# Two attention blocks in fp32 on one core: a fourth convolution in halves twice, the projection straight after attention, and statistics moved

## The chip, the cores and the metric

The program runs on one core of a Trainium2 chip. The core has a matrix engine (TensorE, PE in the profile), three engines for elementwise work (VectorE or DVE, ScalarE or ACT, GpSimd or POOL), a sequencer that issues transfers (SyncE, SP), and 16 DMA engines that its queues share. Each engine takes its instructions in the order of its own queue and waits on semaphores for the others. The metric is the device time of one execution in microseconds (us), here a median over ten executions.

## The reference

The input is a batch of 8 images, each 512 channels by 1024 positions (32 x 32), in fp32. Two attention blocks follow each other:

```python
# layer 0: group norm (32 groups), 8 heads of 64 channels
h   = group_norm(x)
qkv = w_qkv @ h + b_qkv                     # [1536, 1024] per image
weight = softmax((q * s).T @ (k * s))       # per head, [1024, 1024]
a   = weight @ v                            # back to [512, 1024]
x   = x + w_proj @ a + b_proj
# layer 1: group norm (8 groups), one head of 512 channels
xn  = group_norm(x)
q, k, v = q_w @ xn + q_b, k_w @ xn + k_b, v_w @ xn + v_b
attn = softmax(q.T @ k / sqrt(512))         # [1024, 1024]
out  = attn @ v
x    = x + p_w @ out + p_b
```

All that matters here is matrix products of 512 x 512 weights with 512 x 1024 images, the attention products, and the elementwise work between them.

## The kernel before

**Products by halves.** A product of two matrices that are each cut into 2 x 2 blocks is made from seven block products instead of eight, with sums of blocks before and after (`wino`, L227; its seven products carry the numbers 1 to 7). `left_sums` (L151) and `right_sums` (L165) make the sums of the two factors: eight subtractions or additions of 128 x 512 for one image. The weights' sums are made once in the prologue and kept in DRAM (`prepare`, `keep`), and each use reads them back with `load_weight` (1.79 MB) into one of three buffers, three uses ahead in the list `uses`. In `wino`, step p does the matmuls of product p (4 of 128 x 128 by 512 columns for a weight product) and then reads the accumulator that is complete: 1, 2, 5, 6 and 7 run in the order of `middle`, and steps 4 and 3 are put into the list `tail`, which the next product runs behind its own step 1 (`finish`), so that the accumulators of one product are read while the next product's first matmuls run.

**Halves twice.** Two convolutions of layer 0, for keys and queries, go one level further (`conv2`, L416): each of the seven products is itself made from seven, so 49 matmuls of 256 columns take the place of 28 of 512 columns. The inner sums of the image are made by POOL (`inner_factors`, L400; 28 subtractions of 128 x 256, L411), the inner sums of the weights once in the prologue by POOL (`keep2`, L296: four operations of 128 x 896 and seven transfers). `conv2` runs in four groups (`pair`) of products: (1,5), (2,6), (7) and (3,4). In each group the inner steps go 1, 6, 2, 5, 7, and the inner steps 3 and 4 run behind the next group's step 1. Each result is an addition of an accumulator and an earlier result on DVE (`add`, L439); `more` (L444) adds on POOL what product 7 gives to two places. An accumulator holds several results one after the other: step 7 adds onto the accumulator that step 6 left, so its matmuls wait until DVE has read it (the buffer `u`), step 3 onto that of step 5 (buffer `c`), and step 4 onto that of step 7.

**Names in the profile.** The tiles are named by stage: `g` is layer 1's first convolution (the weights `m` are the product of layer 1's query and key weights, made in the prologue), `p` layer 0's projection, `sc` and `av` the scores and the weighted values, `z` layer 1's second convolution, `v`, `k`, `q` layer 0's three convolutions. `psa_`, `psb_`, `psc_` are their accumulators (PSUM), `h` and `t_h` a normed image and its sums, `inner_h` the sums of sums, `a` and `t_a` the output of layer 0's attention and its sums, `bnst` the statistics of a norm.

**The order of the stages.** The loop over images (L928) software-pipelines the two layers. For image b of 1 to 7 it runs: layer 0's attention of image b (`attention0`, L577: eight blocks, one for each pair of heads and half of the queries), then layer 1's first convolution `g` of image b-1, the projection of image b (`projection`), layer 1's scores, `z` and weighted values of image b-1, and layer 0's `v`, `k` and `q` of image b+1. For image 0 it is attention, then image 1's `v`, the projection of image 0, and image 1's `k` and `q`. After the loop, layer 1 of the last image runs alone.

**One attention block** is eight score products, each followed by an exponential on ACT (L594) and, from the second on, by an addition of 128 x 1024 on DVE into the sum (L596, L598); then sixteen products with the values (`av`); then a matmul of the sum with ones (`sums`, L557), which waits for the last of the seven additions, since PE's queue is in order, and the next block's products wait behind it. DVE takes the reciprocal (L559); a row of it goes to DRAM and comes back broadcast (`rows` and `r`, both on SP's queue), and POOL scales the block's output with it (L615). The last block's scaling is done by DVE (`scaled`, L617) inside the stage that follows.

**What sets the order.** Matmuls keep the program's order (L67). On the other engines a scheduler orders what is not pinned by `tc.keep_in_program_order`. The list `background` holds small elementwise steps which `wino` and `conv2` take out between their own steps (`run_background`); the lists `hooks`, `extra` and `later` put steps at given places. The norm of layer 1 takes its statistics inside the projection: `residual` adds the projection to the image (L845, L847), and puts `bn_stats` (L98, eight of 128 x 512 for an image) and `bn_aggr` (L103, four) into `background`; the group's mean and variance go over PE (`gmean`, `gvar`) between the steps of the scores.

Of the kernel before, what the change touches and what calls it, by code (L numbers as in the profile page):

```python
# [29 lines left out]
def two_attention_blocks_kernel(  # L30
# [145 lines left out]
    def main_path(ctx):  # L176
# [117 lines left out]
        wdram2 = {n: dram.tile([P, 7, 7, P], F32, name=f"sums2_{n}") for n in "qk"}  # L294

        def keep2(n, t):  # L296
# [5 lines left out]
            for dst, x, y, op in (  # L302
                (s1, a21, a22, ALU.add), (s2, s1, a11, ALU.subtract), (s3, a11, a21, ALU.subtract),
                (s4, a12, s2, ALU.subtract),
            ):
                nc.gpsimd.tensor_tensor(dst, x, y, op)
# [3 lines left out]
        twice = [("k", 0), ("k", 1), ("q", 0), ("q", 1)]  # L310
        uses = ["v", "p", *twice] if B > 1 else ["p"]
        for b in range(1, B):
            uses += ["m", "p", "z"] + (["v", *twice] if b + 1 < B else [])
# [3 lines left out]
        def load_weight():  # L317
            if uses:
                n = uses.pop(0)
                t = wpool.tile([P, 7 * C], F32, tag="w", name=f"w_{n[0]}_{len(uses)}")  # L320
                if n in twice:
# [18 lines left out]
        def image_factors(h, uid):  # L340
# [5 lines left out]
                [lambda j, t=t: t[:, j, :] for t in tiles], nc.vector.tensor_sub,  # L346
# [69 lines left out]
        def conv2(n, f, bias, name, hooks=(), late=None):  # L416
# [123 lines left out]
            last = [lambda: biased_half(0, 1), lambda: biased_half(1, 0)]  # L540
# [3 lines left out]
            pair(3, (3, 4), [(0, 1), (1, 0)], [(0, 1), (1, 0)], [load_weight, *last])  # L544
# [3 lines left out]
        def reciprocals(total, uid, across):  # L548
# [14 lines left out]
            nc.sync.dma_start(rows.rearrange("j i n -> i j n"), rc[0:P:32, :, :])  # L563
            if across:
                r = pair_tile(f"r_{uid}")
                for j in range(2):
                    row = rows[j : j + 1].rearrange("j i n -> j (i n)")
                    nc.sync.dma_start(r[:, j, :], row.to_broadcast([P, HT]))
            else:
                r = rpool.tile([P, HT], F32, tag="r", name=f"r_{uid}")  # L570
                for j in range(2):
                    row = rows[j : j + 1].rearrange("j i n -> j (i n)")
                    nc.sync.dma_start(r[ts(j, 64), :], row.to_broadcast([64, HT]))
# [3 lines left out]
        def attention0(b, q, k, v, extra):  # L577
            a = channel_tiles(f"a0_{b}")
            n = 0
            for hp in range(KC):  # L580
                for tb in range(2):
# [31 lines left out]
                    r = reciprocals(total, uid, False)  # L613
                    if (hp, tb) != (KC - 1, 1):
                        nc.gpsimd.tensor_tensor(dst, dst, r, ALU.mult)  # L615
                    else:
                        scaled = lambda dst=dst, r=r: nc.vector.tensor_mul(dst, dst, r)  # L617

            assert not extra
            return a, scaled  # L620
# [131 lines left out]
        def prologue():  # L752
# [45 lines left out]
            for n in "pmz":  # L798
                t, steps = prepare(n)
                later.append(steps)  # L800
                later.append([lambda n=n, t=t: keep(n, t), load_weight])
# [5 lines left out]
            return v, q, k, norm1, later  # L807

        psum_pools("first", 2)
        v, q, k, norm0, later = prologue()  # L810
# [23 lines left out]
        def attention_steps(a, scaled, b):  # L834
            af, steps = image_factors(a, f"a_{b}")
            return af, [[], [scaled, lambda: background.extend(steps)]]

        def projection(b, af, xt):

            norm = GroupNorm(1, f"1_{b}")  # L840

            def residual(i, r, c, ps, u):
                oc = 2 * r + i
                xh = xt[oc][:, ts(c, HT)]
                nc.vector.scalar_tensor_tensor(xh, ps, obias[0][:, oc : oc + 1], xh, ALU.add, ALU.add)  # L845
                if u is not None:
                    nc.vector.tensor_add(xh, xh, u)  # L847
                background.append(lambda: norm.half_stats(oc, c, xh))

                if c == 1 - r:  # L850
                    background.append(lambda: norm.end_stats(oc))
# [6 lines left out]
            by_channel(weight("p"), af, f"p_{b}", residual, after=[load_weight, store])  # L858
            return norm

        def norm_hooks(norm, uid):
            return [
                [], [], [all_background], [lambda: norm.group_mean(acc_tile(f"gmean_{uid}")[:, :KC])],
# [28 lines left out]
        def layer1_scores(b, h, hooks):  # L892
            hf, steps = image_factors(h, f"h1_{b}")
            background.extend(steps)
            g = conv(
                weight("m"), hf, ubias, f"g1_{b}", middle=(2, 5, 6, 7), hooks=hooks, back=4,
                after=[load_weight, lambda: background.extend(gsteps)],
            )
# [6 lines left out]
            return hf, gf  # L905

        def layer1_rest(b, hf, gf, hooks, ahead):
            e, total, ef = scores1(b, gf, hf, f"1_{b}", hooks)
# [19 lines left out]
        for b in range(B):  # L928
# [11 lines left out]
            for i, f in enumerate(applies):  # L940
                extra[2 * i + 3].append(f)
            if b > 0:
                extra[0] += late
            psum_pools(f"attention_{b}", 1)
            a, scaled = attention0(b, q, k, v, extra)
            psum_pools(f"products_{b}", 2)
            xt = [load_x(b, c, "x") for c in range(KC)]
            af, ends = attention_steps(a, scaled, b)
            if b > 0:
                hf, gf = layer1_scores(b - 1, h, ends)  # L950
                norm1 = projection(b, af, xt)
# [9 lines left out]
            elif B > 1:  # L961
                v, f, norm0 = values(1, h, ends)
                norm1 = projection(0, af, xt)
                q, k, late = keys_and_queries(1, f, norm0, norm_hooks(norm1, "1_0")[1:])
            else:
                for f in sum(ends, []):
                    f()
                all_background()
                norm1 = projection(0, af, xt)
                finish()  # L970
                for f in sum(norm_hooks(norm1, "1_0"), []):
# [4 lines left out]
        hf, gf = layer1_scores(B - 1, h, ())  # L976
# [197 lines left out]
```

## Time and profile before

| | |
|---|---|
| median of 10 executions | 2904.65 us (2902.1 to 2908.01) |
| the profiled execution's own time | 2907.18 us |
| its span in the trace | 2905.4 us |
| granted TensorE clock | 0.999 |
| PE busy | 2888.4 us (99%) |
| DVE busy | 1936.9 us (67%) |
| ACT busy | 872.7 us (30%) |
| POOL busy | 468.2 us (16%) |
| DMA moved | 267.97 MB, mean 92 GB/s |

Busy time is time with at least one instruction in flight on the engine. A matmul's end is modelled, so PE's records overlap a little, and a matmul that starts late behind a wait can lie in the shadow of the one before. The chain of waits is the chain that ended last, followed back from the last instruction; what stands in it is on the path that sets the end. Matmuls of fp32 appear as two records each. The stages of one image of the loop can be told apart in the trace by their tiles: for image 1, attention ends at 452.1 us, and `g`, `p`, the scores, `z`, `av`, `v`, `k` and `q` end at 690 us, where the next image's attention begins.

### The profile page before, as it was taken

The numbers are of one execution on the slowest core, as the hardware profiler recorded it, in microseconds if no ns is written. First come the engines' busy times: TensorE is split into PE (matmuls) and PEld (weight loads), VectorE is DVE, ScalarE is ACT, GpSimd is POOL, SyncE is SP. The second block draws the span as 40 slices with busy tenths as digits, with TensorE's granted clock in tenths as the row PEclk, the third lists the DMA queues.
The fourth block names the chain that finished last, engine by engine and source line by source line (L and its number), as shares of the span: only waits on it lengthen the run. The fifth ranks groups of instructions, "written<-read, shape, count | busy, mean of one in ns | idle before, by whom it ended". The sixth has DMA issues, their size and how long they took to land.

```text
span 2905.4 us, 29024 instructions
## 1 busy us (share of the span) xinstructions
PE 2888.4 (99%) x10838; PEld 1499.5 (52%) x10838; DVE 1936.9 (67%) x2613; ACT 872.7 (30%) x1117; POOL 468.2 (16%) x525
## 2 busy tenths in 40 slices
PE   9999999999999999999999999999999999999999
PEld 5435634566345653457534574346733458334544
DVE  5488787556765668665786567866577665776555
ACT  1251452114512055121551115411164112631110
POOL 3013210032200322003210122102121031110000
PEclk9999999999999999999999999999999999999999
DMA  8432402133032231222312232122411223011201
GB/s 277 156 133 92 175 19 93 68 123 132 19 112 87 87 126 48 83 92 95 116 47 81 92 135 77 48 80 95 149 62 44 80 103 146 30 55 69 91 3 66
DMA packets 84186, 267.97 MB, mean 92 GB/s; under 512 B 10371, under 2 KB 29891, under 8 KB 75974
## 3 DMA queue, kind: packets, MB, share of 16 engines
q1 hardware_dynamic: 83622, 265.89, 25.3%
q8 instruction: 87, 1.43, 0.2%
q14 instruction: 61, 0.50, 0.1%
q10 hardware_dynamic: 416, 0.16, 0.0%
HBM read 216.30 MB, written 49.72 MB: 92 GB/s over the span
## 4 chain that ended last, share of the span: by engine, by line
PE 98%; DVE 2%; DMA 0%; issue 0%; ACT 0%; SPq 0%; DVEq 0%
PE sc L67 15%; PE av L67 15%; PE psb_sc L67 6%; PE psb_av L67 6%; PE psa_av L67 4%; PE psa_sc L67 4%; PE psc_av L67 4%; PE psc_sc L67 4%; PE psb_p L67 3%; PE psb_z L67 3%; PE psb_g L67 3%; PE psb_v L67 3%; PE psb_k L67 3%; PE psb_q L67 2%; PE psa_v L67 2%; PE psa_z L67 2%
## 5 line engine op out<-in xcount | busy, mean ns | idle before, releaser
L598 DVE TENSOR_TENSOR sum<-sum,e 128x1024 f32<-128x1024 f32 x384 | 519.1, 1352 | 40.4 <-DVE sum L598 0.5
L594 ACT ACTIVATE e<-sc 128x1024 f32<-128x1024 f32 x512 | 476.8, 1050 | 72.8 <-PE sc L67 72.8
L67 PE MATMUL sc<-q,k 64*128 64x512 f32 x2048 | 458.3, 596 | 0.0
L67 PE MATMUL av<-e,v 128*64 128x512 f32 x2048 | 453.6, 595 | 0.0
L67 PEld LDWEIGHTS sc<-q,k 64*128 64x128 f32 x2048 | 192.3, 186 | 239.2 <-ACT e L594 110.1
L67 PEld LDWEIGHTS av<-e,v 128*64 128x64 f32 x2048 | 141.4, 137 | 304.3 <-issue 302.3
L561 POOL TENSOR_TENSOR all_recs<-all_recs,rc 128x256 f32<-128x256 f32 x72 | 64.5, 896 | 883.2 <-DVE rc L559 883.2
L559 DVE RECIPROCAL rc<-sums 128x256 f32<-128x256 f32 x72 | 126.4, 1756 | 89.3 <-PE sums L67 87.0
L615 POOL TENSOR_TENSOR a<-a,r 128x512 f32<-128x512 f32 x56 | 109.3, 1952 | 270.9 <-DMA r<-rows 251.7
L646 ACT ACTIVATE e<-e 128x512 f32<-128x512 f32 x96 | 60.5, 630 | 232.6 <-DVE e L645 232.6
L612 ACT COPY a<-av 128x512 f32<-128x512 f32 x64 | 37.5, 586 | 304.9 <-PE av L67 304.9
L596 DVE TENSOR_TENSOR sum<-e,e 128x1024 f32<-128x1024 f32 x64 | 78.5, 1226 | 60.2 <-ACT e L594 60.2
L67 PE MATMUL psa_sc<-g,h 128*128 128x512 f32 x256 | 115.7, 594 | 0.0
L67 PE MATMUL psa_av<-e,z 128*128 128x512 f32 x256 | 113.3, 595 | 0.0
L128 POOL TENSOR_TENSOR rstd<-ve,mhalf 128x4 f32<-128x4 f32 x16 | 16.7, 1044 | 499.6 <-DVE ve L126 499.6
L140 ACT ACTIVATE h<-h,b,s 128x1024 f32<-128x1024 f32 x62 | 78.5, 1270 | 60.9 <-DMA h<-in_x 48.3
L67 PEld LDWEIGHTS psa_sc<-g,h 128*128 128x128 f32 x256 | 48.1, 190 | 57.9 <-issue 56.2
L67 PEld LDWEIGHTS psa_av<-e,z 128*128 128x128 f32 x256 | 48.0, 190 | 57.3 <-issue 55.2
L67 PE MATMUL psb_k<-inner_h,w_k 128*128 128x256 f32 x294 | 75.3, 383 | 0.0
L67 PE MATMUL psb_q<-inner_h,w_q 128*128 128x256 f32 x294 | 74.9, 383 | 0.0
L249 ACT COPY t_sc<-psa_sc 128x512 f32<-128x512 f32 x32 | 18.7, 586 | 181.7 <-DVE x L847 152.4
L444 POOL TENSOR_TENSOR k<-k,k 128x256 f32<-128x256 f32 x28 | 20.1, 728 | 297.0 <-DVE u_k L439 297.0
(304 smaller groups left out, 4584.4 us busy)
## 6 DMA issues: line engine op xcount, KB each, us to landing
x<-in_x SPq DMA_DIRECT2D x36, 512.0 KB
h<-in_x SPq DMA_DIRECT2D x32, 512.0 KB
r<-rows SPq DMA_DIRECT2D x128, 128.0 KB
spill<-x SPq DMA_DIRECT2D x32, 512.0 KB
h<-spill SPq DMA_DIRECT2D x32, 512.0 KB
x<-spill SPq DMA_DIRECT2D x32, 512.0 KB
out<-x SPq DMA_DIRECT2D x64, 256.0 KB
w_p<-sums_p SPq DMA_DIRECT2D x8, 1792.0 KB
```

Source lines behind the costliest of these rows:

```text
L67: tc.keep_in_program_order(nc.tensor.matmul(*args, **kw))
L140: tc.keep_in_program_order(nc.scalar.activation(dst, src, AF.Identity, bias=b, scale=s))
L249: nc.scalar.copy(t1[i], ps["a", i])
L444: nc.gpsimd.tensor_tensor(d, x, y, ALU.add)
L559: nc.vector.reciprocal(rc, sums)
L561: nc.gpsimd.tensor_tensor(all_recs, all_recs, rc, ALU.add)
L594: nc.scalar.activation(e, sc, AF.Exp, scale=(C // 8) ** -0.5)
L596: nc.vector.tensor_add(total, es[0], e)
L598: nc.vector.tensor_add(total, total, e)
L612: nc.scalar.copy(dst, av)
L615: nc.gpsimd.tensor_tensor(dst, dst, r, ALU.mult)
L646: nc.scalar.activation(dst, dst, AF.Exp, scale=scale)
```

## The change

`m` joins `k` and `q` among the weights with sums of sums, and `g` of images 0 to 6 is made by `conv2`; the last image keeps the plain form. The order after the attention of image b becomes projection of image b, `g` of image b-1, scores. The projection's `middle` becomes (5, 6, 7, 2).

The projection needs all of attention's output soon, so the last pair's two blocks swap, and the block that ends last is (3, 0): its half is part of what products 2 and 4 need, and its scaling (`scaled`) and one last sum come behind step 7. That block's `rows` and `r` transfers go on ACT's queue. The sums of attention's output are pinned and mostly made inside attention's last two blocks. The sums of layer 1's image (`image_factors` of `h1`), which DVE made around the beginning of `g`, are spread over blocks 4 to 7 of attention, and their inner sums (28 operations on POOL) are issued when attention is over, so that they run beside the projection.

The statistics of layer 1's norm are pinned, collected in a list, and put into `background` after the second group of `conv2`; the means and variances move one step earlier in the scores. In `conv2` the last two biased halves swap.

In image 0 the inner sums of the weights `m` are made by `keep2`, now pinned on POOL, after the first attention (`more_later`), followed by the load of `p`, and the statistics of image 0 are taken in image 1's `k`.

```diff
-        wdram2 = {n: dram.tile([P, 7, 7, P], F32, name=f"sums2_{n}") for n in "qk"}
+        wdram2 = {n: dram.tile([P, 7, 7, P], F32, name=f"sums2_{n}") for n in "qkm"}
         def keep2(n, t):
...
-                nc.gpsimd.tensor_tensor(dst, x, y, op)
+                tc.keep_in_program_order(nc.gpsimd.tensor_tensor(dst, x, y, op))
...
         for b in range(1, B):
-            uses += ["m", "p", "z"] + (["v", *twice] if b + 1 < B else [])
+            uses += ["p", *twice["m"], "z"] + (["v", *twice["k"], *twice["q"]] if b + 1 < B else [])
...
-            pair(3, (3, 4), [(0, 1), (1, 0)], [(0, 1), (1, 0)], [load_weight, *last])
+            pair(3, (3, 4), [(0, 1), (1, 0)], [(0, 1), (1, 0)], [load_weight, *last, *after])
...
-        def attention0(b, q, k, v, extra):
-            a = channel_tiles(f"a0_{b}")
+        def attention0(b, q, k, v, a, extra):
...
-                for tb in range(2):
+                for tb in (0, 1) if hp < KC - 1 else (1, 0):
...
-                    r = reciprocals(total, uid, False)
-                    if (hp, tb) != (KC - 1, 1):
+                    last = (hp, tb) == (KC - 1, 0)
+                    r = reciprocals(total, uid, False, nc.scalar if last else nc.sync)
+                    if not last:
                         nc.gpsimd.tensor_tensor(dst, dst, r, ALU.mult)
...
-            norm = GroupNorm(1, f"1_{b}")
+            norm = GroupNorm(1, f"1_{b}", pinned=True)
+            stats, rest = [], []
...
-                background.append(lambda: norm.half_stats(oc, c, xh))
+                stats.append(lambda: norm.half_stats(oc, c, xh))
                 if c == 1 - r:
-                    background.append(lambda: norm.end_stats(oc))
+                    stats.append(lambda: norm.end_stats(oc))
...
+            by_channel(
+                weight("p"), af, f"p_{b}", residual, middle=(5, 6, 7, 2), hooks=[[], [], hooks, [], [add_rest]],
+                after=[load_weight, store],
+            )
+            return norm, stats
...
-        def layer1_scores(b, h, hooks):
-            hf, steps = image_factors(h, f"h1_{b}")
-            background.extend(steps)
-            g = conv(
-                weight("m"), hf, ubias, f"g1_{b}", middle=(2, 5, 6, 7), hooks=hooks, back=4,
-                after=[load_weight, lambda: background.extend(gsteps)],
-            )
+        def layer1_scores(b, hf, inner, hooks):
+            after = [lambda: background.extend(gsteps)]
+            if inner:
+                g = conv2("m", inner, ubias, f"g1_{b}", hooks, after)
+            else:
+                g = conv(weight("m"), hf, ubias, f"g1_{b}", middle=(2, 5, 6, 7), back=4, after=[load_weight, *after])
...
         def layer1_rest(b, hf, gf, hooks, ahead):
+            finish()
             e, total, ef = scores1(b, gf, hf, f"1_{b}", hooks)
...
+            a = channel_tiles(f"a0_{b}")
+            af, steps = image_factors(a, f"a_{b}", lambda *t: tc.keep_in_program_order(nc.vector.tensor_sub(*t)))
+            extra[13] += steps[:2]
+            extra[15] += steps[2:4]
             if b > 0:
                 extra[0] += late
+                hf, sums = image_factors(h, f"h1_{b - 1}")
+                for i in range(4):
+                    extra[9 + i] += sums[2 * i : 2 * i + 2]
...
             if b > 0:
-                hf, gf = layer1_scores(b - 1, h, ends)
-                norm1 = projection(b, af, xt)
+                inner, sums2 = inner_factors(hf, f"h1_{b - 1}")
+                for f in sums2:
+                    f()
+                norm1, stats = projection(b, af, xt, [scaled, steps[7]])
+                gf = layer1_scores(b - 1, hf, inner, [[], [lambda: background.extend(stats)]])
...
             elif B > 1:
-                v, f, norm0 = values(1, h, ends)
-                norm1 = projection(0, af, xt)
-                q, k, late = keys_and_queries(1, f, norm0, norm_hooks(norm1, "1_0")[1:])
+                more_later()
+                v, f, norm0 = values(1, h, [[], [scaled, steps[7]]])
+                norm1, stats = projection(0, af, xt)
+                load_weight()
+                hooks = norm_hooks(norm1, "1_0")
+                hooks[0].append(lambda: background.extend(stats))
+                q, k, late = keys_and_queries(1, f, norm0, hooks)
```

In the order that the scheduler gives the changed kernel's DVE, blocks 4, 5 and 6 of each attention have two of the 128 x 512 subtractions between the sixth and the seventh addition into the sum. The eight `bn_stats` and four `bn_aggr` stand one by one between the additions of `g` that follow the second group's step 7: three `bn_stats` ahead of, between and behind its steps 3 and 4, four among the third group's six additions, one in the last group; the `bn_aggr` stand in the third and last groups.

## The prediction

> **What bounds the kernel now.** I read the page's busy line and the chain of waits first, then PE's timeline of one image (number 1, 452.1 to 690 us), then DVE's beside it.
>
> ```profile
> PE 2888.4 (99%) x10838; PEld 1499.5 (52%) x10838; DVE 1936.9 (67%) x2613; ACT 872.7 (30%) x1117; POOL 468.2 (16%) x525
> ...
> PE 98%; DVE 2%; DMA 0%; issue 0%; ACT 0%; SPq 0%; DVEq 0%
> ```
>
> PE is the chain, and the other engines enter it for 2%. So a matmul taken away is worth its whole time, unless PE then waits; every new wait of PE counts in full. The question of this change is where DVE, at 67% on average, has no room. Two places matter. The first is attention, PE's and DVE's rows of the end of a block and the next one's beginning:
>
> ```profile
> 434.90 1.23 DVE L598 TENSOR_TENSOR sum<-sum,e 128x1024 f32<-128x1024 f32 x1
> 437.68 1.76 DVE L559 RECIPROCAL rc<-sums 128x256 f32<-128x256 f32 x1 [1.55 <-PE sums L67]
> 439.47 0.42 DVE L560 TENSOR_TENSOR low_recs<-low_recs,rc 128x256 f32<-128x256 f32 x1
> 440.64 1.23 DVE L596 TENSOR_TENSOR sum<-e,e 128x1024 f32<-128x1024 f32 x1 [0.74 <-ACT e L594]
> 441.97 8.76 DVE L598 TENSOR_TENSOR sum<-sum,e 128x1024 f32<-128x1024 f32 x6
> 450.64 1.29 DVE L170 TENSOR_TENSOR t_h<-h 128x512 f32<-128x512 f32 x2
> ...
> 451.57 0.64 PE L67 MATMUL sums<-sum,ones 128*32 128x256 f32 x8
> ```
>
> The seven additions run without a gap from 440.64 to 450.73, and the matmul of the sums starts at 451.57: the last addition is 0.84 us early. The subtractions at 450.64 stand behind it and delay nothing. The second place is `conv2`, here keys' third group, one product alone:
>
> ```profile
> 656.61 0.69 DVE L439 TENSOR_TENSOR k<-psb_k,c_k 128x512 f32<-128x512 f32 x1
> 657.90 0.69 DVE L439 TENSOR_TENSOR k<-psc_k,u_k 128x512 f32<-128x512 f32 x1 [0.60 <-PE psc_k L67]
> 658.84 0.76 DVE L439 TENSOR_TENSOR k<-psb_k,k 128x256 f32<-128x256 f32 x2 [0.24 <-PE psb_k L67]
> 659.51 0.41 DVE L439 TENSOR_TENSOR u_k<-psb_k,k 128x256 f32<-128x256 f32 x1
> 659.84 0.41 DVE L439 TENSOR_TENSOR k<-psa_k,k 128x256 f32<-128x256 f32 x1
> 660.17 0.41 DVE L439 TENSOR_TENSOR c_k<-psc_k,k 128x256 f32<-128x256 f32 x1
> 660.72 0.42 DVE L439 TENSOR_TENSOR k<-psb_k,c_k 128x256 f32<-128x256 f32 x1
> ...
> 659.43 0.59 PE L67 MATMUL psc_k<-inner_h,w_k 128*128 128x256 f32 x2
> 659.98 0.70 PE L67 MATMUL psb_k<-inner_h,w_k 128*128 128x256 f32 x2
> ```
>
> From 658.84 to 660.58 DVE has no gap, and PE's step 7 starts at 659.98, when `u_k` (659.51 to 659.92) has read the accumulator, 0.12 late. Here DVE is level with PE without any statistics.
>
> **The change part by part.** S is the time of an attention's last sums matmul.
>
> *The matmuls.* In the chain a 128x256 fp32 matmul is 0.43 us (0.86 for the four records of a two-product step) and a 128x512 one 0.858. `g` goes from 28 x 0.858 = 24.04 to 49 x 0.43 = 21.05: 2.99 less, for images 0 to 6 **-20.9 us**.
>
> *The statistics in `g`.* In the projection DVE has room (18 of 27.5 us busy from 469.5 on), and PE shows no wait there, so taking them out gives nothing. They come back as eight `bn_stats` of 0.68 (one each 0.60 to 0.61 back to back) and four `bn_aggr` of 0.15 to 0.2, each one ahead of an addition whose read PE waits for. I lay them into the keys' timeline in the changed order, with 0.2 us from a matmul's end to DVE and 0.06 back, as those rows show. Step 7's addition of group 2 ends at 657.30. Statistics, then group 2's step 3 (657.94 to 658.63); statistics, step 4 (659.27 to 660.02); statistics, `u` of group 3 (660.63 to 661.05): step 7 starts at 661.1 instead of 659.98. Statistics, step 2 (to 662.06), statistics, `c` (to 663.1): step 3, free to start at 662.5, starts at 663.16; step 4 waits for step 7's addition (663.66) and ends at 664.15. The last group's steps 6, 2, 5 end at 665.0, 666.0, 666.8. On DVE step 3's and 4's additions, two `bn_stats` and two `bn_aggr` run to 666.0, `u` to 666.78, so step 7 goes to 667.7. The last `bn_stats`, step 2's two additions (to 668.15) and a `bn_aggr` stand ahead of `c`, which ends at 669.05; step 3 waits for it from 667.7, because the scores now need `g` and nothing is put between. Step 4 ends at 670.83. Counted from 659.86 (step 5's end) without any wait it would be 659.86 + 7.31 = 667.17. So 3.66 us a time, seven times **+25.6 us**. From below: keys' own wait (0.44) and the short one at the end (0.2), 4.5 us in all. From above: all of the statistics' 8 x 0.61 + 4 x 0.15 = 5.5 on top, 43 us. I take the walk, as its rows are those of the same code. The scores behind it need the biased halves and sums late enough (3.43 us a step against 2 x 0.63 on ACT and 1.25 on DVE).
>
> *Image sums in attention.* In blocks 4, 5 and 6 two subtractions (1.25 together) stand ahead of the seventh addition, which was 0.84 early and is then 0.2 to 0.4 late, with 0.06 to PE; I take 0.25 a block: 3 x 7 x 0.25 = **+5.3 us** (0 if the 0.1 gaps between additions absorb the rest; 21 x 0.47 = 10 at most). Behind the wait stand the next block's scores; DVE itself has 0.74 idle ahead of the next addition.
>
> *Projection straight after attention.* Its step 2 (from S+14.3) needs `scaled`, which waits for the reciprocal (S+0.8 to 2.5), the row's two transfers on ACT's queue (455.41 to 460.67 for the same pair before: 5.2) and then for the subtractions and `u` ahead of it on DVE: S+12.9. Cover 1.4 us: **0**. ACT waits behind its own transfers for nothing urgent. SP loses three issues, the residual images are loaded as before. If the cover is gone, the price is the lateness, below.
>
> *The 28 inner sums on POOL* take 28 x 0.7 = 20 us, to S+25, needed from S+24 on one group at a time: 0. They share a path with DVE's two-input operations: beside such sums before, `o<-o,r` took 0.95 to 1.23 instead of 0.69, 0.26 to 0.54 more, eighteen times out of eighteen, but once this:
>
> ```profile
> 256.00 6.08 DVE L170 TENSOR_TENSOR t_a<-a 128x512 f32<-128x512 f32 x1
> ```
>
> Eight POOL operations passed in that time. I price the projection by the eighteen (three on the path, 1.4 at most, within the cover). [...]
>
> *Image 0.* The four operations of `keep2` (2.08 each by the prologue's row of 8.31 for four) run on POOL from S+4 to S+12.4. Behind them on SP stand the transfers of the sums and the load of `p`, issued at about S+14, and behind 448 KB transfers of about 2 us and with 4.3 us of its own it lands at about S+24, when PE wants it at S+17.8: **+6.7** (4 to 9). Two waits of the old order, 2.9 and 2.1 beside the 6.08 row, go: **-5.0** (0 to -5). Keys of image 1 take the statistics: **+2.3** (half a group earlier on a full PE queue; 0 to 3.7). Sum +4 (-1 to +12).
>
> *Sum:* -20.9 + 25.6 + 5.3 + 4.0 = +14.0. The profiled execution's own time is 2907.2 (span 2905.4 and 1.8 around it), 2.5 above the median; 2907.2 + 14.0 = 2921.2, on the median's footing **2918.7 us**.
>
> **The rivals.**
> *DVE keeps up.* If statistics slip between the additions at no more cost than `q` shows (its chain holds DVE `c_q` for 0.77 behind a norm's small operations, 0.9 with the rest), the third term is 7 x 0.9 = 6.3 and the time 2918.7 - 19.3 = 2899.4, and 2894 if attention also hides its subtractions. For: PE's queue holds steps that do not wait. Against: DVE has 1.74 us without gap exactly there. It decides from a wait in `g` below 2.5 us a time (not slower), below 0.83 (faster).
> *POOL starves DVE every time.* The same order repeats each image, so one 6.08 could repeat too: 5.4 - 1.4 = 4.0, seven times 28 us: 2946.7. For: 28 POOL operations without a pause beside seven two-input ones. Against: one case in some 25 meetings.
> *Only the shorter matmuls count* (both waits hidden, image 0 even): 2904.65 - 20.9 = 2883.8. Against: the two full stretches above.
>
> **How the numbers follow.** A measurement of this kernel tells 0.2%, 5.8 us, from no change: faster is below 2898.8, slower above 2910.5. The walk holds: 0.55, with its own range 2906 to 2932 (g's wait 2.4 to 4.5 a time, attention 0 to 10, image 0). DVE keeps up: 0.25, 2892 to 2908. Starved: 0.12, 2935 to 2955. Only matmuls: 0.08. Leaving out a good half of the last two and the low end of the second: 2895 to 2940. Faster: 0.08 and 0.15 of the second; same: 0.10 and 0.10; slower: 0.45 and 0.12.
>
> **What would show it.** Right: in the changed profile `g`'s 128x256 matmuls take 24 to 25 us from the first to the scores, the chain holds DVE `u_g`, `c_g` and `g` additions of L439; in blocks 4 to 6 PE waits 0.2 to 0.4 for `sum` ahead of `sums`; image 0's projection waits for `w_p` some 7 us. Wrong: `g` ends in 22 us, or a 5 to 6 us subtraction of `a` stands in each projection, or PE waits in the projection for `r`.

## The result

The changed kernel takes 2916.1 us (median of 8 executions, 2915.17 to 2916.66) against 2905.4 us of the kernel before measured beside it (28 executions): a ratio of 1.0038, 95% interval 1.0029 to 1.0046. It is 0.38% slower, clear of the 0.2% that a measurement of this kernel can tell. Forecast were 2918.7 us, with 2895 to 2940 as the range.

The profiled execution took 2915.8 us with a span of 2914.0, 8.6 us longer than the span before. The page's busy line and its chain's line of the changed kernel:

```profile
PE 2878.2 (99%) x11132; PEld 1554.8 (53%) x11132; DVE 2003.7 (69%) x2753; ACT 923.9 (32%) x1201; POOL 683.1 (23%) x781
...
PE 11%; DVE 0%; issue 0%; DVEq 0%
```

The chain breaks off here: it is followed back only to 2578 us, and its shares say nothing of the rest. PE is busy for 10 us less and the span is 8.6 us longer, so PE waits some 19 us more. The view of PE's waits of the changed kernel says for what (us in total, times, the longest):

```profile
PE psb_g L67 <- DVE u_g L439: 5.6, 7, 0.8
PE psc_v L67 <- DVE t_h L170: 5.1, 2, 3.8
PE psc_g L67 <- DVE c_g L439: 5.0, 14, 0.4
PE tr_wk L70 <- DMA rawk<-in_w: 3.8, 1, 3.8
PE sums L67 <- DVE sum L598: 1.4, 7, 0.4
PE psb_v L67 <- DVE u_v L238: 1.4, 1, 1.4
PE psb_k L67 <- DVE u_k L439: 1.1, 1, 1.1
```

Of these only the load of `rawk`, at the very start, was there before. Twenty-one waits lie in the twice-halved `g` (seven images, three each), seven in attention ahead of `sums`, and the others in image 0's stage. The view counts a wait only where it can be seen between records, so the lengths of the stages give the whole. I read them from the first matmul of one stage to the first of the next:

| | before | after | forecast |
|---|---|---|---|
| `g` of images 0 to 6 (7 times) | 169.6 | 165.4 | 174.3 |
| their projections | 168.2 | 169.0 | 168.2 |
| attention's products with the values, images 1 to 7 | 393.0 | 397.9 | 398.3 |
| scores of layer 1 | 339.6 | 341.0 | 339.6 |
| image 0 from the end of attention to the next attention | 97.6 | 103.7 | 101.6 |

Before, `g` and what stands in it took 24.14 us in five images, 24.36 and 24.55 in the other two; after, 23.63. Of the 2.99 us that the shorter matmuls save, 0.6 a time are left on average. Of these 0.1 is no gain: it is the changeover from attention, which the projection now has (24.14 us for 24.03). DVE's rows of the third group of `g`, image 1, in the changed kernel (start, us, engine, line):

```profile
496.95 0.68 DVE L98 BATCH_NORM_STATS2 bnst<-x 128x6 f32<-128x512 f32 x1
497.55 0.41 DVE L439 TENSOR_TENSOR u_g<-psb_g,g 128x256 f32<-128x256 f32 x1
497.88 0.68 DVE L98 BATCH_NORM_STATS2 bnst<-x 128x6 f32<-128x512 f32 x1
498.48 0.41 DVE L439 TENSOR_TENSOR g<-psa_g,g 128x256 f32<-128x256 f32 x1
498.80 0.68 DVE L98 BATCH_NORM_STATS2 bnst<-x 128x6 f32<-128x512 f32 x1
499.40 0.41 DVE L439 TENSOR_TENSOR c_g<-psc_g,g 128x256 f32<-128x256 f32 x1
```

and PE's rows that wait for `u_g` (497.55 to 497.96), for `c_g` (to 499.81) and for the last group's `c_g`:

```profile
498.01 0.70 PE L67 MATMUL psb_g<-inner_h,w_m 128*128 128x256 f32 x2 [0.80 <-DVE u_g L439]
...
499.86 0.70 PE L67 MATMUL psc_g<-h,w_m 128*128 128x256 f32 x2 [0.28 <-DVE c_g L439]
...
505.03 0.70 PE L67 MATMUL psc_g<-h,w_m 128*128 128x256 f32 x2 [0.43 <-DVE c_g L439]
```

From 493.79 to 505.64 DVE goes from one instruction to the next without a gap. In `g` that is the mechanism of the forecast, at the places of the forecast.

### The profile page after: what moved, and what is told of

Its sections match the earlier page's. It is cut to its first block, busy times and chain, and to the rows that moved or that the text cites. A ratio compares the mean times of both kernels' runs of the same rounds, so it can differ in the third digit from the quotient of the medians.

```text
span 2914.0 us, 30246 instructions
## 1 busy us (share of the span) xinstructions
PE 2878.2 (99%) x11132; PEld 1554.8 (53%) x11132; DVE 2003.7 (69%) x2753; ACT 923.9 (32%) x1201; POOL 683.1 (23%) x781
## 5 line engine op out<-in xcount | busy, mean ns | idle before, releaser
L411 POOL TENSOR_TENSOR inner_h<-h,inner_h 128x256 f32<-128x256 f32 x112 | 101.7, 913 | 0.5
L411 POOL TENSOR_TENSOR inner_h<-h 128x256 f32<-128x256 f32 x56 | 54.4, 972 | 151.3 <-PE psc_av L67 151.3
L67 PE MATMUL psb_g<-inner_h,w_m 128*128 128x256 f32 x294 | 75.0, 383 | 5.6 <-DVE u_g L439 5.6
```

The costliest lines, as they stand in the source:

```text
L67: tc.keep_in_program_order(nc.tensor.matmul(*args, **kw))
L411: nc.gpsimd.tensor_tensor(dst, x, y, ALU.subtract)
```

## Experiments

Each run is compared with the kernel before on the same chip; the ratio's 95% interval is in brackets. The theory is that PE's new waits have three separate causes: the statistics ahead of `g`'s additions, two subtractions ahead of the seventh addition in attention, and DVE and POOL holding each other up in image 0. The rivals stand in the expectations.

### The statistics in the scores

```diff
-                gf = layer1_scores(b - 1, hf, inner, [[], [lambda: background.extend(stats)]])
+                gf = layer1_scores(b - 1, hf, inner, ())
...
-                layer1_rest(b - 1, hf, gf, norm_hooks(norm1, f"1_{b}"), ahead)
+                hooks = norm_hooks(norm1, f"1_{b}")
+                hooks[1].extend(stats)
+                layer1_rest(b - 1, hf, gf, [hooks[0], hooks[1], [], *hooks[2:]], ahead)
```

> The statistics of images 1 to 7 are issued in the scores, after g's sums, instead of between the additions of the twice-halved g; nothing else changes. In the changed kernel's trace g takes 23.63 us for image 1 against 21.05 of pure matmuls. Theory (DVE's additions come late behind the statistics, and PE waits for their reads): g falls to 21.1 to 21.7 us, the scores pay 0 to 0.5 us, and the time falls by 7 x 1.6 to 2.4 = 11 to 17 us, to 2899 to 2905. Rival (the twice-halved g waits for something else, ACT's copies, POOL's additions or the missing overlap at its end): g stays at 23 to 23.6 us and the time within 3 us of 2916.

Measured: 2927.2 us, ratio 1.0078 [1.0064, 1.0091], slower than the changed kernel. `g` did fall, from 23.63 to 21.82 us in each of the seven images, as the theory said. But the scores grew from 41.85 to 44.2 us in image 1 and 45.9 in image 2, because the matmul of the norm's mean stood in PE's queue one step after the statistics. The view of PE's waits:

```profile
PE gmean L67 <- DVE mv L103: 14.8, 7, 2.1
PE psc_v L67 <- DVE t_h L170: 5.1, 2, 3.8
```

The waits for `u_g` and `c_g` are gone from the list, and a larger one has taken their place. The scores grew by 23.5 us over the seven images, more than the 14.8 of the wait: by 2.4 in each, and by 1.7 more in four of them, where TensorE's granted clock was 0.50 of full speed for 3.41 us behind the wait. These are the windows behind it in image 1, where the clock stayed, and in image 2, where it fell (after the busy times of the five engines, with their instructions, stands the granted clock as a share of full speed):

```profile
521.20:524.61 3.41, 3.41 (x10) 1.50 (x10) 2.03 (x6) 0.10 (x1) 0.00 (x0) 1.00 0.00 0
877.66:881.07 3.41, 3.41 (x5) 1.35 (x4) 0.90 (x4) 0.00 (x0) 0.00 (x0) 0.50 0.00 0
```

My expectation of 0 to 0.5 us for the scores was wrong: I had fitted the statistics into DVE's idle time but not asked what PE's queue holds for them. The cause of `g`'s waits is settled by `g` itself; the time needed another run (below).

### The image sums behind the last addition

```diff
-                            nc.vector.tensor_add(total, total, e)
+                            tc.keep_in_program_order(nc.vector.tensor_add(total, total, e))
...
-                for i in range(4):
-                    extra[9 + i] += sums[2 * i : 2 * i + 2]
+                for i, fs in ((5, sums[:2]), (7, sums[2:3]), (9, sums[3:5]), (11, sums[5:7]), (13, sums[7:])):
+                    extra[i] = extra[i] + fs if i < 13 else fs + extra[i]
```

The subtractions and both forms of the addition are pinned; the first addition likewise.

> The eight subtractions for layer 1's image in attention are pinned behind the last addition into the sum of blocks 2 to 6, one or two a block, and the additions are pinned too. Theory (two subtractions ahead of the seventh addition make it late for the sums matmul): the blocks whose products with the values take 7.2 to 7.5 us before the sums go back to 7.02, three a time, 0.6 to 0.9 us for each of seven images, 4 to 6 us in all: 2910 to 2912. Rival (the lateness is of the exponentials or of POOL's scaling): no change, 2915 to 2917.

Measured: 2911.3 us, ratio 1.0020 [1.0011, 1.0029], 4.8 us below the changed kernel. The wait of `sums` for DVE is no longer in the list, and every block's products take 7.02 us again; in the changed kernel the excess over 7.02 was 4.9 us in all, so the whole of it came back. This is what stood there, DVE's and PE's rows of block 4 of image 1 in the changed kernel:

```profile
404.31 7.43 DVE L598 TENSOR_TENSOR sum<-sum,e 128x1024 f32<-128x1024 f32 x5
411.65 1.29 DVE L170 TENSOR_TENSOR t_h<-h 128x512 f32<-128x512 f32 x2
412.86 1.22 DVE L598 TENSOR_TENSOR sum<-sum,e 128x1024 f32<-128x1024 f32 x1
...
414.13 0.64 PE L67 MATMUL sums<-sum,ones 128*32 128x256 f32 x8
```

The seventh addition runs behind the two subtractions and ends at 414.08; `sums` starts at 414.13 and not at 413.92, 7.02 us after the first product. Here the delay is too short to show as an idle time; only the stage's length, 7.23 us, tells it.

### Weights' inner sums inside image 0's attention

```diff
-            return v, q, k, norm1, later, lambda: (keep2("m", t), load_weight())
+            later += [[lambda: (keep2("m", t), load_weight())]]
+            return v, q, k, norm1, later, lambda: None
```

> The inner sums of the weights m are made on POOL in the fourth block of image 0's attention instead of after it, and the load of p follows there. In the changed kernel v of image 1 takes 26.7 us for what took 17.4 before, with PE waiting for DVE's subtractions of h. Theory (POOL's 128x896 operations hold DVE's two-input subtractions up at the beginning of v): v goes back to 17.4 to 19 us and attention pays 0 to 3 us: 2907 to 2912. Rival (v's image sums are late in any case because the attention output's sums now stand ahead of them on DVE): v keeps 24 us or more and the time stays within 3 us of 2916.

Measured: 2915.3 us, ratio 1.0037 [1.0023, 1.0051], the same as the changed kernel within the intervals. The first part of `v` fell from 26.7 to 20.8 us, but attention paid 4.8 (10.0, 8.6 and 7.4 us for pieces that take 7.0 or 7.1), since POOL's operations of 128x896 now met DVE's additions (the first of that block took 3.10 us instead of 1.23). The 8.6 are scores of which 3.41 us ran at a granted clock of 0.50, behind a wait of 2.9 for `sums`. So the four operations cost nearly as much in attention as in `v`. The 20.8 us lie between the theory (17.4 to 19) and the rival (24 or more). Of the 3.4 that `v` still takes longer than before, the view of PE's waits has 2.9 for `u_v`, which DVE makes behind image 1's sums; a pair of those takes 2.34 us beside POOL's operations of 128x256 and 1.29 elsewhere.

### The three together

> The three edits together (statistics in the scores, image sums behind the last addition, inner sums of m in image 0's attention). Theory (three waits in different places, all on PE's path): the gains add up, 14 + 5 + 6 = 25 us, 2886 to 2896, below the kernel before (2905). Rival (they share a cover, so that one wait takes another's place): 2900 or more.

Measured: 2919.4 us, ratio 1.0049 [1.0035, 1.0062]. Neither the theory's 2886 to 2896 nor below the kernel before, for the reason found in the first run: the scores take 44.2 us, 45.9 in two images. `g` took 21.82 us and the products of attention in images 1 to 7 took 7.02 us a block here too, so two of the gains did add up. The third was none here: `v`'s first part takes 23.7 us, 3.0 less than in the changed kernel, and image 0's attention pays 4.7.

### Statistics in the scores, means in z

The edit adds to the second run the first one's, and moves the norm's two matmuls:

```diff
-                layer1_rest(b - 1, hf, gf, norm_hooks(norm1, f"1_{b}"), ahead)
+                hooks = norm_hooks(norm1, f"1_{b}")
+                layer1_rest(b - 1, hf, gf, [[], hooks[1] + stats], ahead, hooks[2:])
...
-                weight("z"), hf, f"z1_{b}", hooks=[[], [], [], [], [sums]], back=3,
+                weight("z"), hf, f"z1_{b}", hooks=[*norms, [], [], [sums]], back=3,
```

> Beside the image sums behind the last addition (that run took 2911.3 us), the statistics are in the scores and the matmuls of the norm's mean and variance in z's first two steps, so that PE's queue does not wait for the statistics. Theory (the statistics in the scores are free, and the run with the means in the scores lost only by PE's wait of 2.1 us for the mean and what follows it): g takes 21.8 us and the scores 41.8 to 42.3, 7 x 1.3 to 1.8 = 9 to 13 us less than 2911.3: 2898 to 2902. Rival (DVE has no room in the scores either): scores of 43 us or more, 2905 or more.

Measured: 2898.7 us, ratio 0.9985 [0.9976, 0.9994], faster than the changed kernel and, by 0.06 to 0.24%, than the kernel before; that is 4.4 us by the medians, less than the 5.8 that the prediction asked for before it called a kernel faster. `g` takes 21.82 us, the scores 41.40, and `z` 0.4 us more for the two small matmuls that it now holds. Against the second run that is 12.6 us less (10 by the two ratios), and the stages give the 7 x 1.81 that `g` lost. PE's and DVE's rows of the same place in this kernel show what a statistics-free third group looks like:

```profile
496.00 0.41 DVE L439 TENSOR_TENSOR u_g<-psb_g,g 128x256 f32<-128x256 f32 x1
496.33 0.41 DVE L439 TENSOR_TENSOR g<-psa_g,g 128x256 f32<-128x256 f32 x1
496.67 0.41 DVE L439 TENSOR_TENSOR c_g<-psc_g,g 128x256 f32<-128x256 f32 x1
...
496.47 0.70 PE L67 MATMUL psb_g<-inner_h,w_m 128*128 128x256 f32 x2
```

`u_g` has read its accumulator at 496.41, and step 7 follows at 496.47, 0.12 us later than PE was free for it.

### The plain g

The kernel of the run above, with `g` of all images by the plain convolution and without the 28 inner sums on POOL:

```diff
-            uses += ["p", *twice["m"], "z"] + (["v", *twice["k"], *twice["q"]] if b + 1 < B else [])
+            uses += ["p", "m", "z"] + (["v", *twice["k"], *twice["q"]] if b + 1 < B else [])
...
-                inner, sums2 = inner_factors(hf, f"h1_{b - 1}")
-                for f in sums2:
-                    f()
...
-                gf = layer1_scores(b - 1, hf, inner, ())
+                gf = layer1_scores(b - 1, hf, None, ())
```

> As the run with the statistics in the scores and the means in z, but g of images 0 to 6 is the plain convolution (28 matmuls of 512 columns), without the inner sums of the image on POOL. It prices the twice-halved g alone. Theory (49 matmuls of 256 columns are worth 24.04 - 21.05 = 2.99 us, of which 0.8 goes to DVE's reads at the groups' ends): 7 x 2.2 = 15 us longer than the run beside it, 21 us if no such reads count. Rival (the shorter matmuls bring nothing): the same time.

Measured: 2913.3 us, ratio 1.0036 [1.0022, 1.0050], 14.6 us longer than with the twice-halved `g`: 2.1 us an image. The shorter matmuls bring what they should, less what DVE's reads at the groups' ends take back even without any statistics (21.82 - 21.05 = 0.77 an image; in the run above PE's matmuls lose 0.2 us behind `u_g` of the third group, 0.1 behind its next reads and 0.3 behind `c_g` of the last). The scores take 0.2 us an image less here than behind the twice-halved `g`.

### Every statistic twice

The changed kernel with each `bn_stats` issued twice into the same place, which changes no value:

```diff
                 stats.append(lambda: norm.half_stats(oc, c, xh))
+                stats.append(lambda: norm.half_stats(oc, c, xh))
```

> The changed kernel with every bn_stats of layer 1's norm issued twice into the same place, sixteen instead of eight among the additions of g. Theory (in g DVE has no slack, so each bn_stats of 0.60 us that stands ahead of an addition of the last two groups delays PE by about that): 3 to 4.8 us an image, seven times and once for image 0: 24 to 38 us, 2940 to 2954. Rival (DVE has slack and the waits are of another kind): 0 to 8 us, up to 2924.

Measured: 2937.3 us, ratio 1.0118 [1.0103, 1.0134], 21 us above the changed kernel, short of the theory's 24 to 38 and far from the rival's 8. `g` grew from 23.63 to 25.45, 1.82 an image and not 3 to 4.8. The order of DVE's instructions tells why: of the eight more, only three stand ahead of the last group's read of `c`; the other five come behind it, where they cost little. Three times 0.60 is 1.8. The other 8.5 us are in image 1's `k`, which holds the statistics of image 0 and takes 29.55 instead of 21.07 us, 3.8 of them a wait for the mean, as in the first run, and 1.1 more for `u_k`; the granted clock was 0.50 there for 10.24 us from 312.5 on, which is most of the rest:

```profile
PE gmean L67 <- DVE mv L103: 3.8, 1, 3.8
PE psb_k L67 <- DVE u_k L439: 2.2, 1, 2.2
```

### Image 0

Three runs tried to take back the 6 us of image 0 on top of the run with the means in `z`. In the first, DVE makes the inner sums of `m` behind the last addition of blocks 3, 4, 5 and 7 of image 0's attention, and image 1's sums there too:

```diff
-            return v, q, k, norm1, later, lambda: (keep2("m", t), load_weight())
+            parts = keep2("m", t, nc.vector.tensor_tensor)
+            later += [[] for _ in range(9)]
+            for i in (7, 9, 11, 15):
+                later[i].append(lambda: next(parts))
+            later[15] += [lambda: next(parts), load_weight]
+            return v, q, k, norm1, later, lambda: None
...
+                hf, sums = image_factors(h, "h0_1", lambda *t: tc.keep_in_program_order(nc.vector.tensor_sub(*t)))
+                for i in range(4):
+                    extra[7 + 2 * i] = extra[7 + 2 * i] + sums[2 * i : 2 * i + 2] if i < 3 else sums[6:] + extra[13]
```

> The same, and in image 0's attention the inner sums of the weights m are made by DVE behind the last addition of blocks 3, 4, 5 and 7 instead of by POOL behind the attention, and image 1's sums (eight subtractions) in blocks 3 to 6. Theory (in image 0 the time is lost because POOL's 128x896 operations and DVE's two-input operations hold each other up while v waits for the image's sums): v goes from 26.7 to 17.4 to 18.5 us and attention pays 0 to 1.5: 7 to 9 us less than the run beside it, 2890 to 2895. Rival (v waits for the load of p's weights or for its own matmuls' order): v keeps 24 us or more, no gain.

Measured: 2898.1 us, ratio 0.9981 [0.9972, 0.9990]; against the run beside it no difference (2898.7). The first half of `v` did go from 26.7 to 17.37 us, and attention paid 1.3, as the theory said. But 7.3 us came back in `v`'s second half (14.2 for 6.9), 5.2 of them one wait:

```profile
PE psc_v L67 <- DVE v L376: 5.2, 1, 5.2
```

The granted clock was 0.50 for 6.83 us from 265.4 on, which is most of the rest. DVE's rows say what `v` stood behind, a load of the image after the next, that arrives 4 us after DVE is ready for it:

```profile
261.22 1.29 DVE L98 BATCH_NORM_STATS2 bnst<-ahead 128x6 f32<-128x512 f32 x2 [4.09 <-DMA ahead<-in_x]
```

So I moved the last inner sum a block earlier, to let that load go earlier, and took image 0's statistics inside its projection again (those of the halves that get their last addition late, behind it):

```diff
-            for i in (7, 9, 11, 15):
+            for i in (7, 9, 11, 13):
...
-                norm1, stats = projection(0, af, xt)
+                norm1, _ = projection(0, af, xt, stats=background)
```

> As the run with image 0's edits, with two differences: the last of the four inner sums of m stands in block 6 of image 0's attention instead of block 7, so that the load of p and, behind it on SP's queue, the next image's loads are issued a block earlier; and image 0's statistics are taken in its projection as before, not in image 1's k. In that run v no longer waited for its sums (17.4 us), but v's additions on DVE stood behind bn_stats of a late load, and PE waited 5.2 us. Theory (that wait came from the order of the loads, and the statistics cost k 1.8 us as they cost g): v's second part goes from 14.2 to 9 to 10 us, k from 21.1 to 19.3 to 19.7, 5 to 7 us less than 2898.1: 2891 to 2893. Rival (the loads are late because the DMA engines are full, not because of the order): only k gains, 2896 to 2897.

Measured: 2899.5 us, ratio 0.9985 [0.9976, 0.9994], no gain. The statistics were worth 1.2 us in `k` (19.84 after 21.06), and the load was there in time (its `bn_stats` at 258.11). But the scaling behind it was held up, and with it `v`, whose parts take 19.1 and 15.2 us:

```profile
260.01 6.40 DVE L620 TENSOR_TENSOR a<-a,r 128x512 f32<-128x512 f32 x1
```

The theory of the order of the loads was right for the load and wrong for the time: a second wait of the same length (5.3 us) stood behind the first.

In the third the last scaling went to POOL, ahead of its inner sums, and the loads of image 2 into block 5:

```diff
-                    if not last:
+                    scaled = lambda: None
+                    if not last or b == 0:
...
+                extra[11].append(lambda: xs.extend(load_x(2, c, "ahead") for c in range(KC)))
```

> From the run with image 0's statistics in its projection: the loads of image 2 that v's background statistics wait for are issued in block 5 of image 0's attention, ahead of the load of p; the last inner sum of m is back in block 7; and the last scaling of image 0's attention is done by POOL, ahead of its 28 inner sums, so that no operation of DVE with two inputs in SBUF but one stands beside those. In the run before, that scaling took 6.40 us on DVE (0.69 alone) while POOL's inner sums ran one behind the other, v's additions stood behind it, and PE waited 5.3 us. Theory (the starved scaling is the wait): v's second part goes from 15.2 to 9.8 to 10.5 us, k stays at 19.8: 5 to 7 us less than 2899.5, 2892 to 2895. Rival (another two-input operation of DVE is starved in its place): an operation of over 3 us in v and no gain, 2897 or more.

Measured: 2903.5 us, ratio 1.0002 [0.9993, 1.0011], 4 us longer than the run before it by the medians (1.1 by the profiled spans). No operation was starved, and `v`'s second part takes 6.9 us again, as `k` keeps its 19.8. But its first part takes 29.6: the broadcast reciprocals came late, and the last sum of attention's output, which `v`'s first additions stood behind, waited for POOL:

```profile
255.43 1.26 POOL L619 TENSOR_TENSOR a<-a,r 128x512 f32<-128x512 f32 x1 [12.76 <-DMA r<-rows]
...
256.73 1.20 DVE L968 TENSOR_TENSOR t_a<-a,t_a 128x512 f32<-128x512 f32 x1 [10.86 <-POOL a L619]
```

PE waited 10.1 us. The transfers took until 255.4, with the reciprocal done at 241.6. ACT's queue, which issues them, did not hold them up: its last copy ended at 243.4, and it then stood idle until it issued `r` at 247.6, which needs the row to have landed. The DMA engines were full in this time, with loads of weights issued at 239.4 and 242.4 ahead of the row:

```profile
241.60:252.80 11.20, 10.87 (x51) 9.22 (x49) 4.20 (x8) 1.66 (x3) 0.90 (x1) 1.00 1.00 386
```

The last two numbers are the engines' share and the GB/s. That points to the loads; no run moved them. In each of the three runs another wait stood behind the one that was cleared (the sums, the load, the scaling, the reciprocals), and none cleared all of them.

## Why the prediction was right

The forecast sum was +14.0 us; the spans differ by 8.6 and the medians by 10.7. Its sign held, and in `g` and in attention its mechanism and its places. The statistics were sized too high and the scores left at nothing, and image 0's term came near by luck. Of the signs named, the waits for `u_g`, `c_g` and `sum` came (the chain, which breaks off, cannot show them; the view of waits does), `g` took 23.6 us where 24 to 25 were named, and image 0's wait for `w_p` did not come. None of the signs of being wrong came.

**The matmuls, -20.9.** Right: the plain `g` in the same kernel is 14.6 us longer, and 20.0 with the 0.77 an image added that DVE's reads take back.

**The statistics in `g`, +25.6.** Right in mechanism (with the statistics elsewhere, `g` falls by 1.81 a time, and twice the statistics raise it by 0.60 for each one that stands ahead of the last group's `c`). The size was 18.1: 23.63 - 21.05 = 2.58 a time instead of 3.66, and 0.77 of it is there without statistics, so that theirs alone is 12.7. What the walk mis-sized is DVE's pace. I gave every addition the duration of its row, 0.41, 0.69 and 0.75; back to back an addition of 128x256 starts the next instruction 0.32 us later (497.55 to 497.88), one of 128x512 0.61. Thirteen additions at 0.08 to 0.1 make 1.1 us, which is the difference; no run tests it apart. For `bn_stats` I had used the spacing, for the additions not.

**Image sums in attention, +5.3.** Right: 4.9 by the stage's length, all of it given back when the sums stand behind the addition.

**The projection straight after attention, 0.** Right: 24.14 us against 24.03, and the 0.1 is the changeover from attention. POOL's 28 inner sums stretch DVE's operations there by 0.4 to 0.6 (`t_a<-a,t_a` 1.21 instead of 0.68), as the forecast took from the eighteen meetings before, and the cover held. The rival of a starved DVE in each image did not come, but it came once in another kernel, below.

**Image 0, +4.** The size is near, 6.1 by the stage, but that is luck: the step that gave +6.7 did not reach PE. The load of `p` was about as late as I had said; its packets, the only ones of 14336 bytes in that time, ran from 256.3 to 262.3, S+25.5 (6.0 us where I had taken 4.3; the 49 transfers of that size in the kernel before took 4.5 to 7.6). But PE wanted it at 264.0 and not at S+17.8, because `v`, which stands ahead and which I had left at its old length, took 26.7 us for 17.4, and the longer lateness hid the other. What cost the time in `v`: POOL's `keep2` and DVE's two-input subtractions held each other up (2.40 to 2.52 us an operation of POOL for 2.08 in the prologue, 2.55 to 2.56 a subtraction for 0.68), so that image 1's sums, which stand behind those of attention's output on DVE, came 3.8 and 1.3 us late and `u_v` 1.4. With `keep2` elsewhere 5.9 of the 9.3 us went, with image 1's sums moved too all of them. These are POOL's and DVE's rows there in the changed kernel:

```profile
240.24 9.95 POOL L306 TENSOR_TENSOR prepare_m<-prepare_m 128x896 f32<-128x896 f32 x4
250.16 1.17 POOL L411 TENSOR_TENSOR inner_h<-h 128x256 f32<-128x256 f32 x1
...
243.23 2.56 DVE L959 TENSOR_TENSOR t_a<-a,t_a 128x512 f32<-128x512 f32 x1
245.71 5.03 DVE L170 TENSOR_TENSOR t_h<-h 128x512 f32<-128x512 f32 x2
```

A subtraction of 0.68 took 2.55 beside an operation of 128x896. In the prediction I had the 0.26 to 0.54 us that `o<-o,r` took longer beside the inner sums of 128x256; I used them for the projection and did not ask what the four long operations would do. The three waits are 6.5 of the 9.3 us; most of the rest is that the matmuls between and behind them ran at a granted clock of 0.50 of full speed:

```profile
247.09:253.92 6.83, 4.34 (x9) 3.02 (x10) 6.83 (x5) 0.00 (x0) 6.83 (x6) 0.50 1.01 338
```

The 2.9 and 2.1 us that I said would go did go, but only the first was a wait. In the kernel before, PE's list of waits has one there, and a stretch at a granted clock of 0.50 stands behind it, in which four records of 128x512 matmuls take 0.85 us each instead of 0.43, 1.7 of the 2.1 us:

```profile
PE psb_p L67 <- DVE v L375: 2.7, 1, 2.7
...
269.40:272.81 3.41, 3.41 (x5) 1.35 (x4) 3.41 (x7) 0.00 (x0) 0.00 (x0) 0.50 0.11 44
```

`k` took 1.8 more where I said 2.3.

**The scores** pay 0.2 us an image that I had at nothing, 1.4 in all; with the plain `g` they do not.

The rivals: that DVE keeps up is refuted by 21 waits in `g`; that only the matmuls count, by the same.

## What to carry to other kernels

A shorter stage on the busiest engine is worth its time only if the engine that empties its accumulators has that much room in the same stage (here 0.6 of 2.99 us were left): read the second engine's rows of exactly that stretch, not its average. Work that fits a free engine's idle time still costs if something in the bound engine's own queue waits for it (the mean in the scores, 2.1 us a time); move the consumer as well as the work. A wait of some 2 us of the busiest engine can cost more than its length: behind four of the seven waits for the mean the granted clock was 0.50 of full speed for 3.41 us, and there the scores took 4.1 us more, in the other three images 2.4. Two subtractions ahead of the addition that the bound engine waits for cost as much as their lateness (7.23 us for 7.02 in block 4 of image 1), and the same two behind it cost nothing (7.02).

## What the runs showed of the hardware

DVE's operations with two inputs in SBUF took longer beside POOL's sums, and POOL's took longer with them. In the changed kernel four of DVE's of 128x512 took 2.55 to 2.56 us beside POOL's operations of 128x896 (0.68 alone), and POOL's 2.40 to 2.52 (2.07 to 2.09 in the prologue); each of DVE's four ended 0.54 to 0.56 us behind one of POOL's. Of the 127 others that lie beside POOL's sums of 128x256, 114 took 0.94 to 1.29 us, with POOL's at 1.17 in the median where they take 0.72 alone, and 13 took 0.68 as alone. DVE's operations of 128x512 that read an accumulator took 0.67 to 0.75 us beside the same sums, as alone, and its `bn_stats` 0.64 to 0.70.

Twice it went further: 6.08 us in the kernel before (`t_a`, at 256.00) and 6.40 in one experiment (`a<-a,r`, at 260.01). In the second, POOL's rows of the time are these:

```profile
259.65 0.75 POOL L412 TENSOR_TENSOR inner_h<-h,inner_h 128x256 f32<-128x256 f32 x1
260.34 0.75 POOL L412 TENSOR_TENSOR inner_h<-h 128x256 f32<-128x256 f32 x1
261.02 1.43 POOL L412 TENSOR_TENSOR inner_h<-h,inner_h 128x256 f32<-128x256 f32 x2
262.38 0.75 POOL L412 TENSOR_TENSOR inner_h<-h,h 128x256 f32<-128x256 f32 x1
263.07 0.75 POOL L412 TENSOR_TENSOR inner_h<-h,inner_h 128x256 f32<-128x256 f32 x1
```

POOL's operations ran here one behind the other at 0.75 us, as they had ahead of 260.01, while DVE's lasted; in the kernel before eight of 0.72 or 0.73 ran in the 6.08 us. Both were in the same stage, `v` of image 1. In the traces of the kernel before and the changed one 184 operations of DVE of 128x512 with two SBUF inputs lie beside one of POOL's sums (of 128x256 or 128x896), and the one of 6.08 is the only one above 2.56. What sets the two apart stays open.

The granted clock fell to 0.50 at long waits of PE. Between 20 us and the last matmul it was 0.50 in one stretch of the kernel before and in one of the changed kernel, and 1.00 in the rest: for 3.41 us from 269.40 on, 1.7 us behind a wait of 2.7 us that ended at 267.71, and for 6.83 us from 247.09 on, at a wait of 3.8 us that ended at 248.32. At the changed kernel's waits of 1.4 us, to 260.46, and 1.1, to 310.68, it stayed at 1.00. Among the experiments it was 0.50 for 3.41 us behind the 2.9 us for `sums`, for 6.83 us at the 5.2 us in `v`, and for 10.24 us at the 2.2 and 3.8 us in `k` with every statistic twice. Of the seven waits for the mean in the first run, 2.1 us each, four had 3.41 us at 0.50 behind them and three had none. What decides for waits of equal length stays open.
